# Two decoder layers on one core: part of layer 0's vector work moved to other engines, two key heads and two batches handled together

## The chip, the cores and the metric

The kernel runs on one core of a Trainium2 chip. The core has five engines with a queue each, worked off in order: TensorE (PE, with its weight loads PEld), VectorE (DVE), ScalarE (ACT), GpSimd (POOL) and SyncE (SP, which here only issues DMAs). The metric is the device time of one execution in microseconds (us); lower is better. Three runs of the kernel before gave 3500.85 us (median; 3487.28 to 3511.13).

## The reference, cut to what matters

The input is x, 16 batches of 256 tokens of width 256, in float32. Four blocks follow each other; each takes the layernorm of x and adds its result to x.

```python
x = x + attention0(layernorm(x))   # 32 query heads of 8 numbers, 8 key heads, rotary, causal softmax
x = x + experts(layernorm(x))      # a shared expert, and 8 others weighted by the two best logits
x = x + attention1(layernorm(x))   # gated delta rule, 16 heads of 128
x = x + ffn1(layernorm(x))         # gate, up and down weights are lut[index], a table of 16 values
```

For each token the experts give `shared(x) + sum over e of combine[e] * (silu(x @ Wg[e]) * (x @ Wu[e])) @ Wd[e]`, where `combine` is the softmax over the two best of 8 router logits and zero for the others. "Layer 0" below is the first two blocks, "layer 1" the third, "ffn" the last. The change is in layer 0 and in the layernorm helper, which the ffn uses too.

## The kernel before, in words

**Tiling.** x stays in SBUF as 32 tiles of 128 tokens; a batch is two tiles. Products that need more than one pass of 16 bits are made of pairs (a high part and the rest), three matmuls for each two halves of the rows (helper `three`, L114).

**Streams of layer 0.** Everything in layer 0 is written as generators that yield after each step. For each batch there are six: `prepare` (L402: layernorm, queries, keys, values), `greatest` (L461: the greatest score of each query), `attention` (L506), `ready` (L615: layernorm for the experts, then `route`, L564), `experts` (L622) and `to_gates` (L714: the next layer's layernorm and its decays and betas, `gates`, L293). Besides these run `lookups` (L189), which builds the ffn's weights with one-hot matmuls, and the loading of weights. `weave` (L54) issues their steps in the order of planned times in units of one batch: `STREAMS` at L723, with other times for the last two batches in `TAIL` (L725). A scheduler of the framework then places the instructions of each engine in its own order. That order is fixed when the program is built; an engine that waits holds up everything behind the waiting instruction.

**PSUM.** Layer 0 has 8 banks: 3 of role `s` (scores, routing), 3 of role `m` (projections, values, lookups, gates), 1 of role `e` (an expert's gate and up products, `pgu`) and 1 of role `y` (the experts' sum). So only one expert's `pgu` exists at a time, except for the last batch, whose `pgu` uses the three `s` banks.

**An expert** (`up`, L629; `down`, L649). TensorE makes `pgu` in 12 matmuls; ScalarE takes tanh of the gate half (L638); VectorE forms `(tanh + 1) * up` (L640) and times the gate (L641), which is the last to read `pgu`; GpSimd multiplies by the routing weight `cb`, which a DMA has spread over the partitions (L643; not for the shared expert); ScalarE rounds to float16 (L111) and VectorE takes the rest (L112), from SBUF; TensorE adds the two parts' products with the down weights into `ye` (L653). The next expert's `pgu` is issued before this expert's `ye`.

**Attention.** For each of 8 key heads, scores `t` are exponentiated twice by ScalarE (L519, L522), GpSimd subtracts (L523), and TensorE multiplies with the values into `po` (L533). VectorE then sums three parts (L536), inverts the sum of the weights (L539) and multiplies (L540), once for each key head.

**Layernorm helper** `normed` (L93): statistics on VectorE (L100 to L102), the power on GpSimd (L88), then one `tensor_scalar` of 256 elements for each tile on VectorE (L107), from SBUF to SBUF.

**Lookups** (L219 to L237). For each block of columns one matmul of 24 columns gives three parts of 8 results side by side (L234), and VectorE adds the three parts (L235).

**Routing and gates** are done for one batch at a time: 20 small VectorE instructions in `route`, most of 2 to 16 elements, 11 in `of` of `gates`.

Of the kernel before, what the change touches and what calls it, by code (L numbers as in the profile page):

```python
# [10 lines left out]
F32 = mybir.dt.float32  # L11
# [11 lines left out]
P = 128  # L23
B, S, D = 16, 256, 256          # batches, tokens of each, width
NT = B * S // P                 # 32 token tiles
NSB = NT // 4                   # 8 superblocks of 512 tokens
EPS = 1e-5
# layer 0 attention
H0, KV0, HD0 = 32, 8, 8
SC0 = HD0 ** -0.5  # L30
# layer 0 experts
NE, INTER0 = 8, 128
# layer 1 attention
# [3 lines left out]
XS = 2.0**12                    # scale of X and T of layer 1  # L37
WS, NS, OS, HS = 2.0**13, 2.0**10, 20.0, 0.5     # largest weight, and scales of the layernorms and of gated outputs, in pairs of float16
# [3 lines left out]
# layer 1 ffn  # L42
INTER1, NLUT = 688, 16
LOOKED_UP = (("gidx", INTER1, D), ("uidx", INTER1, D), ("didx", D, INTER1))      # rows and columns of the indices
# [9 lines left out]
def weave(*parts):  # L54
    """Issue some steps of each of several streams of work, each spread evenly over a part of the time."""
    turns = sorted((lo + (hi - lo) * (k + 0.5) / n, at, g) for at, (g, n, lo, hi) in enumerate((*x, 0, 1)[:4] if len(x) == 2 else x for x in parts) if g is not None for k in range(n))
    for _, _, g in turns:
        next(g, None)
# [3 lines left out]
def kernel(ctx: ExitStack, tc: tile.TileContext, a, out):  # L62
# [23 lines left out]
    def rsqrt_(t, n):  # L86
        """t [P, n] -> t ** -0.5, in place."""
        POOL.tensor_tensor(t, t, neghalf[:, :n], ALU.pow)  # L88
# [4 lines left out]
    def normed(pool, name, tiles, xn, scale):  # L93
        """xn = the layernorms of a few tiles, times scale."""
# [3 lines left out]
        rs = pool.tile([P, 4], F32, tag="ln_rs", name=f"rs_{name}", bufs=2)[:, :n]  # L98
# [5 lines left out]
        if scale != 1:  # L104
            DVE.tensor_scalar(rs, rs, scale, None, ALU.mult)
        for i, t in enumerate(tiles):
            DVE.tensor_scalar(xn[i], x[:, t, :], mv[:, i, 0:1], rs[:, i : i + 1], ALU.subtract, ALU.mult)  # L107

    def halve(pair, src):
        """pair = two of fewer bits that add up to src."""  # L110
# [3 lines left out]
    def three(ps, l, r):  # L114
        """ps = the products of the pairs l and r over both halves of their rows, less that of the low parts."""
# [4 lines left out]
    def normed_pair(pool, tiles, tag, bufs, bank, dt=F32R, scale=1):  # L120
        """Layernorms of two or four tiles, transposed, times scale, as a pair: [P, 2, 256 or 512]."""
# [17 lines left out]
    def greatest_of(p, bank, ts, name, sizes=()):  # L139
        """The greatest magnitude in each of a few lists of parts, whose rows have a size, on every partition: [P, n]."""  # L140
# [23 lines left out]
    def scales(p, most, name, bufs=2):  # L164
        """Of each weight, its scale, and the inverse of that and of the layernorms' scale."""
# [7 lines left out]
    def split(pair, t, scale):  # L173
        """pair = t times scale in two parts."""
# [3 lines left out]
    def now(g):  # L178
        """All of g at once; what it returns."""
# [6 lines left out]
    # ffn weights of layer 1, looked up on chip and kept in DRAM until they are used  # L186
    wl = {k: dram.tile([cols, rows], F32, tag=f"wl_{k}", name=f"wl_{k}") for k, rows, cols in LOOKED_UP}

    def lookups(pool, bank):  # L189
        """With a partition for each of 16 values and 8 parts of the rows, one or zero where a row's index is  # L190
        its value or not, times the value's entry in three parts: columns of the looked-up rows."""
# [9 lines left out]
        parts = small("parts", [R, 3], BF16)  # L201
        DVE.tensor_scalar(entry, entry, lut[:, 0:1], None, ALU.mult)
        DVE.tensor_copy(parts[:, :, 0], entry)
        DVE.tensor_tensor(rest, entry, parts[:, :, 0], ALU.subtract)
        DVE.tensor_copy(parts[:, :, 1], rest)
        DVE.tensor_tensor(parts[:, :, 2], rest, parts[:, :, 1], ALU.subtract)
# [12 lines left out]
        for name, rows, cols in LOOKED_UP:  # L219
            n = rows // R  # L220
            for c in range(0, cols, P):
# [4 lines left out]
                for k0 in range(0, n, step):  # L226
# [5 lines left out]
                    ps = bank(f"lk_{name}_{c}_{k0}")[:m, : ks * R * 3].rearrange("p (k r n) -> p r k n", k=ks, n=3)  # L232
                    for k in range(ks):
                        PE.matmul(ps[:, :, k, :], lhsT=hot[:, k * m : (k + 1) * m], rhs=parts, start=True, stop=True)  # L234
                    DVE.tensor_reduce(w[:, :, k0 : k0 + ks], ps, AX.X, ALU.add)  # L235
# [7 lines left out]
    # layernorms, transposed, in pairs; by head the decays of each position (zero for the first of a  # L243
    # chunk), and from the start of a chunk to each position
# [5 lines left out]
    def weights(j, p, one, stage):  # L250
        """Those of group j."""
# [15 lines left out]
        # of the values: no more than 1024 afterwards  # L267
# [20 lines left out]
        # scale of the gated outputs (no more than 2^16 then), and that of their products with the weights  # L288
# [4 lines left out]
    def gates(p, one):  # L293
        """What gives, for a batch, its part of beta, xd, al_d and dc_d."""
# [10 lines left out]

        def of(b):
            xT = normed_pair(p, range(2 * b, 2 * b + 2), "xT3", 1, one, F16, NS)
            for d, t in zip(xd[b // 2], xT):
                nc.sync.dma_start(out=d[:, :, b % 2 * S : b % 2 * S + S], in_=t)
            yield  # L310
            pz = one(f"gz_{b}")[:, : 4 * H1].rearrange("p (i n) -> p i n", i=2)
            for i in range(2):
                three(pz[:, i, :], [t[:, :, i * P : (i + 1) * P] for t in xT], bgk)
            parts = p.tile([P, 4, 2, 2 * H1], F32, tag="ga", name=f"ga_{b}", bufs=1)
# [934 lines left out]
```

## Time and profile before

| what | us |
|---|---|
| three runs, median (range) | 3500.85 (3487.28 to 3511.13) |
| profiled execution, its span from first to last instruction; no other time of it is given | 3504.0 |
| layer 0: until layer 1's first matmul | 1262 |
| last layer 0 attention output added to x (L560) | 1198.8 |
| last experts' output added to x (L664) | 1242.5 |
| layer 1: until the last output added to x (L1091) | 1262 to 3277 |
| ffn | 3278 to 3504 |
| VectorE busy, all | 2790.1 |
| TensorE busy, all | 2962.5 |
| ScalarE busy, all | 2107.7 |
| GpSimd busy, all | 1817.1 |

A group line of the profile reads: source line, engine, operation, tile written and tiles read, shapes, count; then busy time and mean ns of one instruction; then the idle time of that engine just before, and who ended it. A tile line gives shortest, median and longest duration in ns. A stage line (busy time of each engine in a stretch) gives the stretch, its length, then busy us and number of instructions of PE, PEld, DVE, ACT and POOL, then the granted TensorE clock as a share of full speed, the DMA engines' share and GB/s.

### The profile page before, as it was taken

What the parts mean: (1) busy time and instruction counts of PE and PEld (TensorE: products, weight loads), DVE (VectorE), ACT (ScalarE), POOL (GpSimd) and SP (SyncE); (2) the same over time, 40 slices, a digit from 0 to 9 for tenths busy, and PEclk for the clock granted to TensorE, in tenths of its full rate; (3) what the DMA queues carried; (4) which work ended last, traced back from release to release, by engine and by line L of the source; (5) the groups of instructions that cost most, each with busy time, mean ns of one, the idle gap of its engine ahead of it and who ended that gap; (6) DMA issues with size and microseconds to landing.
All of it is one profiled execution on the core that took longest, in us unless ns stands there. A gap on an engine that the chain in (4) does not pass through costs nothing.

```text
span 3504.0 us, 74239 instructions
## 1 busy us (share of the span) xinstructions
PE 2962.5 (85%) x28806; PEld 2346.1 (67%) x28806; DVE 2790.1 (80%) x5697; ACT 2107.7 (60%) x5131; POOL 1817.1 (52%) x1631
## 2 busy tenths in 40 slices
PE   3577877777778858989999899999989999999799
PEld 3356656556556636777777777777777777777688
DVE  4689988998889768888888888888888888887432
ACT  1455655555566536776776767676676676767332
POOL 2456555555556444555555555555555555554232
PEclk7789989999999968999999999999999999999899
DMA  6412222222232120111111111111111111110000
GB/s 178 134 58 69 76 74 76 82 68 81 73 81 53 34 69 16 55 52 47 34 40 39 57 48 36 40 32 52 42 51 40 32 40 35 37 35 13 25 25 25
DMA packets 175744, 188.60 MB, mean 54 GB/s; under 512 B 20734, under 2 KB 133214, under 8 KB 173662
## 3 DMA queue, kind: packets, MB, share of 16 engines
q1 hardware_dynamic: 166030, 167.07, 16.8%
q10 hardware_dynamic: 9360, 16.79, 1.6%
q8 instruction: 225, 3.69, 0.4%
q14 instruction: 129, 1.06, 0.1%
HBM read 150.14 MB, written 32.02 MB: 52 GB/s over the span
## 4 chain that ended last, share of the span: by engine, by line
PE 31%; DVE 19%; DMA 5%; ACT 4%; issue 2%; POOL 2%; SPq 0%; ACTq 0%; DVEq 0%; POOLq 0%
PE pr L850 5%; DMA Dm<-al_d 4%; DVE acc L865 3%; PE pq L899 3%; DVE Dm L932 3%; PE g L850 3%; DVE X L983 2%; PE Z L981 2%; DVE XT L961 2%; PE fg L118 2%; PE fu L118 2%; PE fy L777 2%; PE Y L975 2%; PE y L1089 2%; DVE XT L989 1%
## 5 line engine op out<-in xcount | busy, mean ns | idle before, releaser
L523 POOL TENSOR_TENSOR el<-e,eh 128x512 f16<-128x512 f32 x384 | 450.9, 1188 | 193.4 <-ACT eh L522 130.0
L865 DVE SCALAR_TENSOR_TENSOR acc<-pr,cv,acc 128x510 f32<-128x510 f32 (+2 forms) x384 | 281.2, 734 | 76.0 <-ACT acc L861 71.9
L519 ACT ACTIVATE e<-t 128x512 f32<-128x512 f32 x384 | 231.1, 603 | 139.5 <-PE t L517 70.4
L956 POOL TENSOR_TENSOR Tf<-Dm,kkm 128x512 f32<-128x512 f32 x128 | 161.7, 1282 | 246.7 <-DVE kkm L950 238.5
L983 DVE CAST_PREDICATED X<-masks,Z 128x512 f16<-128x512 uint8 x320 | 220.4, 689 | 67.3 <-PE Z L981 67.0
L522 ACT ACTIVATE eh<-t 128x512 f16<-128x512 f32 x384 | 229.0, 602 | 28.1 <-PE po L533 27.8
L1082 POOL TENSOR_TENSOR gl<-sg,gh 128x512 f16<-128x512 f32 x128 | 159.1, 1243 | 159.7 <-ACT gh L1081 156.3
L977 ACT ACTIVATE Y<-Y 128x512 f16<-128x512 f32 x320 | 191.1, 597 | 74.5 <-PE Y L975 73.4
L932 DVE TENSOR_TENSOR_SCAN Dm<-Dm,bI 128x512 f32<-128x512 f32 x128 | 184.2, 1440 | 56.9 <-DMA Dm<-al_d 53.0
L981 PE MATMUL Z<-Y,XT 128*128 128x64 f16 x2560 | 208.1, 249 | 24.5 <-ACT Y L977 20.6
L88 POOL TENSOR_TENSOR f<-f,neghalf 128x4 f32<-128x4 f32 x128 | 149.3, 1166 | 125.2 <-DVE f L1068 123.0
L981 PEld LDWEIGHTS <-XT 128*128 128x128 f16 x2560 | 176.1, 122 | 54.2 <-issue 31.8
L850 PE MATMUL pr<-xT,wqkv 128*128 128x512 f16 x768 | 208.2, 411 | 2.6 <-ACT v L907 2.6
L930 POOL TENSOR_TENSOR bI<-ident,beta 128x512 f32<-128x512 f32 x128 | 134.8, 1054 | 133.3 <-DVE Dm L932 100.4
L850 PEld LDWEIGHTS <-wqkv 128*128 128x128 f16 x1152 | 118.5, 111 | 119.7 <-issue 36.8
L850 PE MATMUL g<-xT,wga 128*128 128x256 f16 x1536 | 196.8, 279 | 1.9 <-DVE acc L865 0.8
L643 POOL TENSOR_TENSOR h<-h,cb 128x256 f32<-128x256 f32 x128 | 95.8, 749 | 192.9 <-DVE h L641 77.7
L515 PE MATMUL t<-Qt,Kt 128*128 128x512 bf16 x384 | 150.8, 402 | 51.9 <-DVE nm L486 31.3
L1089 PE MATMUL y<-woa,gh 128*128 128x256 f16 x1024 | 183.0, 275 | 8.0 <-ACT gh L1081 5.7
L975 PE MATMUL Y<-X,Th 128*128 128x64 f16 x2560 | 145.6, 202 | 44.2 <-DVE X L983 33.9
L486 DVE TENSOR_REDUCE nm<-s 128x2 f32<-128x512 f32 x256 | 171.7, 677 | 13.7 <-PE s L485 13.2
L989 DVE STREAM_TRANSPOSE XT<-X 128x512 f32<-128x512 f32 x256 | 179.6, 702 | 1.9
(362 smaller groups left out, 9930.9 us busy)
## 6 DMA issues: line engine op xcount, KB each, us to landing
Dm<-al_d SPq DMA_DIRECT2D x128, 256.0 KB
cb<-cd SPq DMA_DIRECT2D x128, 128.0 KB
dB<-dc_d ACTq DMA_DIRECT2D x64, 256.0 KB
xT<-xd SPq DMA_DIRECT2D x64, 256.0 KB
Qt<-qd SPq DMA_DIRECT2D x32, 408.0 KB
qd<-both SPq DMA_DIRECT2D x32, 192.0 KB
xr_gidx<-ix_gidx SPq DMA_DIRECT2D x34, 160.0 KB
xr_uidx<-ix_uidx SPq DMA_DIRECT2D x34, 160.0 KB
```

The costliest lines, as they stand in the source:

```text
L519: ACT.activation(e32, ps, AF.Exp, scale=SC0)
L522: ACT.activation(eh[n], ps, AF.Exp, scale=SC0)
L523: POOL.tensor_tensor(el[n], e32, eh[n], ALU.subtract)
L850: PE.matmul(ps, lhsT=r if flip else l, rhs=l if flip else r, start=k == 0, stop=k == len(todo) - 1)
L865: DVE.scalar_tensor_tensor(to[:, :, d:], frm[:, :, : S - d], w["cv"][:, ct, 3 - d : 4 - d], to[:, :, d:], ALU.mult, ALU.add)
L932: DVE.tensor_tensor_scan(flat(Dm[c]), flat(Dm[c]), flat(bI), 0.0, ALU.mult, ALU.add)
L975: PE.matmul(py[:, c, h, :], lhsT=Th[c][:, h, :], rhs=even(X)[:, h, :, :, c], start=True, stop=True)
L977: ACT.activation(Y, py, AF.Copy, scale=XS**-2)
L981: PE.matmul(pz[:, h, :, c], lhsT=XT[:, h, :, c], rhs=Y[:, c, h, :], start=True, stop=True)
L983: DVE.copy_predicated(even(X).rearrange("p h n e c -> p h n (e c)"), bcast(odd[s_].rearrange("p (n e) c -> p n (e c)", e=s_), 1, G), split ...
L989: DVE.transpose(words(XT), words(X))
L1089: PE.matmul(py, lhsT=pair[m][:, h, :], rhs=w["wo"][n][:, h, :], start=k == 0, stop=k == len(todo) - 1)
```

## The change

Line numbers of the new version are about 5 to 30 higher. It does the following:

1. `normed`: VectorE makes `shift = -mean * rs` in one small instruction for each call, and ScalarE makes `x * rs + shift` for each tile (activation Identity with a bias and a scale taken from SBUF); the VectorE instruction L107 is gone, here and in the ffn.
2. `lookups`: the three parts are added by TensorE, three matmuls of 8 columns in place of one of 24; ScalarE copies the sum out of PSUM in place of VectorE's sum.
3. `values` of the attention: two key heads share one PSUM bank; one sum, one inverse (written back into PSUM) and one product for both.
4. `ready`, `route` and `gates` take one batch, (0), then six pairs (1,2) to (11,12), then 13, 14 and 15 each alone.
5. `experts`: GpSimd's product with `cb` comes before VectorE's second product, whose result is written into the up half of `pgu` in PSUM; ScalarE and VectorE make the two float16 parts from there. So `pgu` is in use until L112 is done, not until L641.
6. The planned times of `ready`, `experts`, `gates` and of the last four batches change.

```diff
-        rs = pool.tile([P, 4], F32, tag="ln_rs", name=f"rs_{name}", bufs=2)[:, :n]
+        rs, shift = (pool.tile([P, 4], F32, tag=f"ln_{k}", name=f"{k}_{name}", bufs=2)[:, :n] for k in ("rs", "shift"))
...
+        DVE.scalar_tensor_tensor(shift, mv[:, :n, 0], -1.0, rs, ALU.mult, ALU.mult)
         for i, t in enumerate(tiles):
-            DVE.tensor_scalar(xn[i], x[:, t, :], mv[:, i, 0:1], rs[:, i : i + 1], ALU.subtract, ALU.mult)
+            ACT.activation(xn[i], x[:, t, :], AF.Identity, bias=shift[:, i : i + 1], scale=rs[:, i : i + 1])
...
                     for k in range(ks):
-                        PE.matmul(ps[:, :, k, :], lhsT=hot[:, k * m : (k + 1) * m], rhs=parts, start=True, stop=True)
-                    DVE.tensor_reduce(w[:, :, k0 : k0 + ks], ps, AX.X, ALU.add)
+                        for h in range(3):
+                            PE.matmul(ps[:, k], lhsT=hot[:, k * m : (k + 1) * m], rhs=parts[:, h], start=h == 0, stop=h == 2)
+                    ACT.copy(w[:, :, k0 : k0 + ks], ps.rearrange("p k r -> p r k"))
...
-            def values(g, eh, el):
-                po = bank(f"po_{b}_{g}", "v")[:, :200].rearrange("p (i h n) -> p i h n", i=2, h=4)
+            def values(g, eh, el, po):
+                g2 = g % 2
...
+                if g2 == 0:
+                    return
...
-                DVE.reciprocal(rinv, po[:, :, :, 0])
+                DVE.reciprocal(po[:, :, :, 0], po[:, :, :, 0])
+                at = 32 * (g - 1)
                 DVE.tensor_tensor(
-                    on[:, :, 32 * g : 32 * g + 32].rearrange("p i (h d) -> p i h d", d=8), sums, bcast(rinv, 3, 8), ALU.mult)
+                    on[:, :, at : at + 64].rearrange("p i (h d) -> p i h d", d=8), sums, bcast(po[:, :, :, 0], 3, 8), ALU.mult)
...
-        def route(b, xT):
+        def route(bs, xT):
...
                 DVE.scalar_tensor_tensor(h, h, 1.0, pgu[:, 1], ALU.add, ALU.mult)
-                DVE.scalar_tensor_tensor(h, pgu[:, 0], 0.5 * HS / (WS * NS) ** 2, h, ALU.mult, ALU.mult)
                 if e < NE:
                     POOL.tensor_tensor(h, h, cb, ALU.mult)
+                DVE.scalar_tensor_tensor(pgu[:, 1], pgu[:, 0], 0.5 * HS / (WS * NS) ** 2, h, ALU.mult, ALU.mult)
                 pair = [p.tile([P, S], F16, tag=f"h{m}", name=f"h{m}_{b}_{e}") for m in range(2)]
-                halve(pair, h)
+                halve(pair, pgu[:, 1])
...
-        STREAMS = ((prepare, 7, -3.4, -2.4), (greatest, 26, -1.7, -0.55), (attention, 34, 0, 0.9), (ready, 5, 1.3, 1.75), (experts, 28, 1.75, 2.65), (to_gates, 3, 2.65, 3.15))
+        STREAMS = ((prepare, 7, -3.4, -2.4), (greatest, 26, -1.7, -0.55), (attention, 34, 0, 0.9))
+        TOGETHER = [(0,)] + [(b, b + 1) for b in range(1, B - 3, 2)] + [(b,) for b in range(B - 3, B)]
+        READY, EXPERTS, GATES = (5, 1.15, 1.5), (28, 1.5, 2.4), (3, 3.3, 3.8)
+        TAIL = {
+            B - 4: ((1.15, 1.5), (1.5, 2.35), (3.2, 3.6)), B - 3: ((1.3, 1.6), (2.2, 2.95), (2.95, 3.2)),
+            B - 2: ((1.25, 1.5), (1.95, 2.6), (2.6, 2.8)), B - 1: ((0.97, 1.15), (1.6, 2.2), (2.2, 2.4))}
         LOOK, LOAD, EXW, GTW = (120, 1, 16), (26, 5, 16), (31, -2.4, 1), (3, 1, 1.2)
-        TAIL = {B - 2: ((1.2, 1.5), (1.5, 2.3), (2.3, 2.6)), B - 1: ((0.95, 1.1), (1.1, 1.9), (1.9, 2.2))}
...
+        for bs in TOGETHER:
+            b, n = bs[-1], len(bs)
+            (r0, r1), (e0, e1), (g0, g1) = TAIL[b] if b in TAIL else (READY[1:], EXPERTS[1:], GATES[1:])
+            todo.append((ready(bs), READY[0], b + r0, b + r1))
+            for k in range(n):
+                at = b + e0 + k * (e1 - e0)
+                todo.append((experts(bs[k]), EXPERTS[0], at, at + e1 - e0))
+            todo.append((to_gates(bs), GATES[0], b + g0, b + g1))
```

## The prediction

> **What bounds the kernel now.** I read the stage table first, since the change only touches layer 0 and the layernorms of the ffn. Columns: stretch, length, then busy us of PE, PEld, DVE, ACT, POOL.
>
> ```profile
> 0.00:263.00 263.00, 147.99 (x1261) 106.94 (x1262) 172.75 (x406) 97.14 (x185) 112.55 (x113) 0.79 0.44 123
> 263.00:1139.00 876.00, 696.61 (x7438) 524.64 (x7437) 780.67 (x2077) 503.93 (x1024) 507.69 (x481) 0.93 0.27 73
> 1139.00:1262.00 123.00, 85.99 (x829) 64.26 (x827) 79.92 (x249) 57.66 (x122) 50.12 (x56) 0.85 0.16 43
> 1262.00:3278.00 2016.00, 1820.71 (x18066) 1465.76 (x18066) 1670.47 (x2779) 1378.68 (x3685) 1075.04 (x925) 0.96 0.13 40
> 3278.00:3504.00 226.00, 211.15 (x1216) 184.52 (x1216) 86.32 (x189) 70.25 (x117) 71.66 (x59) 0.95 0.09 29
> ```
>
> In the main stretch of layer 0, 263 to 1139, VectorE is busy 781 of 876 us (89%), TensorE 80%, ScalarE and GpSimd 58%. In the ffn TensorE is busy 93% and VectorE 38%: what VectorE saves there (32 instructions L107) buys nothing. Layer 1 is not touched. So the question is what layer 0's 1262 us become.
>
> Second, the groups of instructions inside layer 0.
>
> ```profile
> L523 POOL TENSOR_TENSOR el<-e,eh 128x512 f16<-128x512 f32 x384 | 450.9, 1188 | 193.4 <-ACT eh L522 130.0
> ...
> L112 DVE TENSOR_TENSOR h<-h,h 128x256 f16<-128x256 f32 x144 | 87.1, 605 | 22.7 <-ACT h L111 22.3
> ...
> L540 DVE TENSOR_TENSOR on<-sums,rinv 128x64 f32<-128x64 f32 x128 | 71.0, 555 | 0.3
> L107 DVE TENSOR_SCALAR xn_xT<-x,mv_xT,rs_xT 128x256 f32<-128x256 f32 x96 | 63.6, 701 | 3.6 <-POOL el L523 1.3 <-PE xnp_xT L131 1.1 <-POOL rs_xT L88 0.8
> ...
> L536 DVE TENSOR_REDUCE sums<-po 128x64 f32<-128x192 f32 x128 | 44.0, 344 | 1.5 <-PE po L533 1.3
> ```
>
> Third, the expert's own tile (shortest/median/longest ns), because the change lengthens the use of the only `pgu` bank.
>
> ```profile
> L638 ACT ACTIVATE h<-pgu,half_down x144: 448/473/624, 225.6 to 1235.8; 128x256 f32<-128x256 f32 x144
> L640 DVE SCALAR_TENSOR_TENSOR h<-h,pgu x144: 356/408/423, 227.1 to 1236.5; 128x256 f32<-128x256 f32 x144
> L641 DVE SCALAR_TENSOR_TENSOR h<-pgu,h x144: 361/412/425, 227.6 to 1238.1; 128x256 f32<-128x256 f32 x144
> L111 ACT CAST h<-h x144: 387/406/550, 228.4 to 1239.6; 128x256 f16<-128x256 f32 x144
> L112 DVE TENSOR_TENSOR h<-h,h x144: 351/416/1856, 229.0 to 1240.9; 128x256 f16<-128x256 f32 x144
> L643 POOL TENSOR_TENSOR h<-h,cb x128: 717/727/922, 233.3 to 1238.6; 128x256 f32<-128x256 f32 x128
> ...
>   POOL h L643: 75.2, 39
> ...
>   PE pgu L118: 23.2, 21
> ```
>
> Two things are seen. L112 and L640 have the same 256 elements; L640 and L641, with an operand in PSUM, never take over 425 ns, L112, all in SBUF, takes up to 1856, a mean of 605. The surplus is about the 1188 ns of one GpSimd instruction L523: VectorE instructions of this kind stand still while GpSimd works. L540 (203/496/1667) and L107 (352/414/1810) show the same. And the first `pgu` product of the next expert starts in the middle case 0.33 us after L641 ends (start times of the trace): the one bank is reused at once.
>
> **The change part by part, VectorE in layer 0** (busy 172.75 + 780.67 + 79.92 = 1033 us).
> - L107 goes: −63.6. `shift` for 36 calls (16 `prepare`, 10 `ready`, 10 `gates`, where 48 calls were): nearest row L318, a small product of two SBUF tiles, 436 ns: +16. Twelve calls fewer also save L102 and L105 (256 and 469 ns): −9.
> - L235 goes: 9.8 + 8.9 + 8.8 = −27.5.
> - Two key heads at once: L536, L539 and L540 cost 44.0 + 24.6 + 71.0 = 139.6. After: 64 times (sum: L235 shows 120 elements in 260 ns against 192 in 344, so 1.2 ns an element, 344 + 230 = 574; inverse 200; product 203 + 67 = 270, free of the standing still because one operand is in PSUM) = 67. −72. If the product still stands still: 64 x (555 + 67) = 40 instead of 17, so −49 at least.
> - Routing: the 20 instructions of one batch sum to 6.4 us, gates' 11 to 3.4 us; six calls fewer of each, less the longer rows (0.5 and 0.4 each): −35 and −18.
> - L112 reads PSUM: 144 x (605 − 412) = −28. [...]
>
> Sum: −63.6 + 16 − 9 − 27.5 − 72 − 35 − 18 − 28 = −237 us, bounds −200 and −250: VectorE falls to about 796.
>
> **What the others get.** ScalarE: 96 scalings; tanh with one scale from SBUF takes 475 for 256 elements, and L861 (scale from SBUF, 512 elements) takes 84 more than L519 (none), so a second operand makes 560: +54. 110 copies like L319 (258) : +28. Table loads fall from 34 to 22 in the program, 12 x 1.283 = −15; fewer gates −8. Sum +59 on 659. That is 61% of the time forecast below, so it is hidden, except in the layernorm's own chain (560 for 414 ns). TensorE: 536 matmuls become 1608; five of them took 0.28 us in the timeline, the first 0.175, so 26 ns each: 1072 x 0.026 = +28 (each alone: 175 ns, +188; they follow each other, so 28). GpSimd: 12 powers fewer, −9. SP's queue: 18 DMAs fewer; `cd` goes out once for two batches. Its loads of `cb` wait there for GpSimd's product to free the buffer (188.5 us, 65 times, in the waits of SP), and others stand behind them; that product comes earlier in an expert now, so this wait doesn't grow by the change alone.
>
> **What is lengthened.** (a) `pgu` stays in use through GpSimd's product, L641, L111 and L112. In the undisturbed expert at 1202.1 the next `pgu` came 3.04 us after this one, with L112 ending 1.62 us after that. So the least cycle is 3.04 + 1.62 and a wake of 0.05 = 4.7 us. (b) VectorE now waits for GpSimd in the middle of an expert; today that wait (75.2 us, 39 times) is ScalarE's. Behind it on VectorE stand the `nm` sums that free the score banks, and TensorE waits for those. (c) A pair is routed only when its second batch has its attention, so experts come later: in TensorE's order 20 experts stand behind the last attention output instead of 13.
>
> **Sum, by the expert's cycle.** Experts follow each other without gap because of the one bank, so they are the clock of layer 0. Before: 225.6 to 1199 for 131 experts, 7.43 us each; the unhindered cycle is 3.0, so 4.4 us of it is queueing at four hand-overs. After: the order of each engine in the built programs shows four experts in every pair of batches (18) with nothing else on TensorE between them; those take 4.9. For the other 14: between L640 and L641 two VectorE instructions stand in both programs (median), between L641 and L112 seven before and two after, 0.38 us each on average (780.67/2077). Part of that runs beside GpSimd's and ScalarE's own shares of the chain, so I take 0.4 us of queueing at each of seven hand-overs: 4.7 + 2.7 = 7.4. At the pair's end gates wait for the experts, about 3 us. So (14 x 7.4 + 4 x 4.9 + 3)/18 = 7.0 us. Attention ends at 225 + 124 x 7.0 = 1093 instead of 1199. Behind it: 11 experts on the one bank x 4.9 = 54, six more of the last batch on three banks x 2.3 (today's nine take 21.8) = 14, a rest of 2: 70 us where 1199 to 1243 were 44. Then 19 us to layer 1, as before. Layer 0 ends at 1182 instead of 1262: −80.
>
> Can TensorE follow? Of its 697 us in the main stretch, 7 experts (15 us) move behind the attention and 28 come: 710 us, in 876 − 106 = 770 us: 92%, where layer 1 reaches 90%. At 90% the stretch takes 789, attention ends at 1112, layer 0 at 1201: −61. [...] Weight loads are 525 + 28 − 9 = 544 us, 71% of 770, where layer 1 shows 73%: at 73% the stretch could go down to 745, layer 0 to 1157: −105. Busy time says that −80 is a little too much, weight loads that it is not. I take the middle of −80 and −61: the profiled execution at 3504 − 71 = 3433; it lies 3 us above the median of the runs, so 3430.
>
> **The rivals.**
> 1. *The bank eats the gain.* The change then does what it says to VectorE, and it buys nothing. With 0.5 us at each of the seven hand-overs instead of 0.4 the 14 take 8.2, the mean is 4.9 x 4/18 + 8.2 x 14/18 + 0.2 = 7.6: 225 + 124 x 7.6 + 89 = 1256, −6: 3495. One tenth of a us for each hand-over is the whole gain. For it: the 0.33 us after which the bank is reused today. Against: the tighter order, and a VectorE at 68%.
> 2. *Slower.* VectorE waits for GpSimd (b), whose product may stand behind L523 (1188 ns) or a late `cb` (22.8 us in all today), and the `nm` sums wait with it, then TensorE's scores. It decides at 124 x c + 314 = 1262, c = 7.65; 0.6 us a hand-over makes 8.9 and c = 8.2: 225 + 1017 + 89 = 1331, +69: 3570. For it: seven hand-overs for four, and today each costs 1.1. Against: VectorE has 237 us to spare, and the wait is 75 today.
> 3. *More.* At 0.25 us a hand-over the 14 take 6.45, the mean 6.3: 225 + 781 + 89 = 1095; weight loads allow 1157 or, at TensorE's ffn share of 82% (184.52/226), 663 for the stretch. Between 1110 and 1150: about 3375. [...] Against: 80% busy today.
>
> **Numbers.** Forecast 0.48, rival 1 0.25, rival 2 0.17, rival 3 0.10. About 1% (35 us) is what a measurement of this kernel can tell from no change. The forecast (c from 6.75 to 7.35, so 3390 to 3464) and rival 3 are faster: 0.58; rival 1 is the same: 0.25; rival 2 slower: 0.17. The range of 8 in 10 goes from 3375 (half of rival 3 lies below) to 3540 (most of rival 2 lies above); the forecast's own is 3390 to 3464.
>
> **What would show it.** Right: VectorE near 795 busy in layer 0; L112 of the experts near 0.41 without long ones; the mean from tanh to tanh near 7.0 until the last attention output, which lands near 1093 to 1112; 70 us behind it. Wrong: VectorE idle before the second gate product, with GpSimd named, over 75 us; TensorE idle before `pgu`, with L112 named, over 100 us; or a layer 1 or ffn that moves by over 10 us.

## The result, and the profile after

The changed kernel took 3654.4 us (median of four runs, 3651.0 to 3658.2), the kernel before 3500.5 us beside it: ratio 1.044, 95% interval 1.0414 to 1.0466. It is 4.4% slower. The forecast was 3430, the range ended at 3540. The profiled execution has a span of 3649.2 us; it is 145 us longer than that of before. The stage table shows where (columns as in the prediction):

```profile
0.00:263.00 263.00, 152.28 (x1406) 108.79 (x1407) 162.40 (x380) 111.04 (x218) 118.70 (x118) 0.81 0.45 126
263.00:1295.00 1032.00, 798.35 (x8721) 591.72 (x8721) 655.80 (x1626) 549.72 (x1206) 517.50 (x491) 0.86 0.23 63
1295.00:1385.00 90.00, 61.33 (x413) 42.84 (x410) 39.76 (x130) 27.97 (x61) 15.12 (x21) 0.83 0.12 31
1404.00:3419.00 2015.00, 1814.05 (x18066) 1462.54 (x18066) 1667.55 (x2782) 1379.98 (x3685) 1073.89 (x925) 0.96 0.14 40
3419.00:3649.00 230.00, 213.73 (x1216) 185.59 (x1216) 76.16 (x165) 85.86 (x149) 70.52 (x59) 0.95 0.09 28
```

Layer 1 took 2015 us (2016 before), the ffn 230 (226). All of the loss is in layer 0: the last attention output lands at 1294.6 instead of 1198.8 (+96), and from there to the last experts' output it takes 90 instead of 44 us (+46). In the main stretch (263 to 1295) no engine is busy for most of the time any more: VectorE 656 of 1032 us (64%; it was 89%), TensorE 77%, ScalarE and GpSimd 53 and 50%. So the added time is waiting, and the question is for what.

The expert's own instructions are as short as foretold. Shortest, median and longest ns, by the tile `h`:

```profile
L653 ACT ACTIVATE h<-pgu,half_down x144: 449/474/609, 216.8 to 1380.5; 128x256 f32<-128x256 f32 x144
L655 DVE SCALAR_TENSOR_TENSOR h<-h,pgu x144: 359/421/423, 217.3 to 1381.5; 128x256 f32<-128x256 f32 x144
L658 DVE SCALAR_TENSOR_TENSOR pgu<-pgu,h x144: 360/426/433, 218.4 to 1382.8; 128x256 f32<-128x256 f32 x144
L112 ACT CAST h<-pgu x144: 350/373/442, 219.2 to 1383.3; 128x256 f16<-128x256 f32 x144
L113 DVE TENSOR_TENSOR h<-pgu,h x144: 386/416/426, 220.0 to 1383.7; 128x256 f16<-128x256 f32 x144
L657 POOL TENSOR_TENSOR h<-h,cb x128: 718/726/939, 223.1 to 1382.0; 128x256 f32<-128x256 f32 x128
```

L113 (L112 before) has no long ones left: 426 at most, where it had 1856. But look at the waits of layer 0 in the kernel after (who waited, for whom; us in total, times, longest):

```profile
POOL h L657 <- DVE h L655: 197.4, 63, 8.6
ACT h L653 <- PE pgu L119: 171.8, 102, 5.3
DVE h L655 <- ACT h L653: 156.2, 88, 5.3
...
ACT h L112 <- DVE pgu L658: 93.3, 57, 3.6
...
PE ye L668 <- ACT h L112: 72.8, 43, 2.6
...
DVE pgu L658 <- POOL h L657: 43.5, 45, 3.8
```

Each step of the expert is named as what the next engine sat idle for. In the kernel before the same view has only these of the expert among its first eight rows:

```profile
POOL h L643 <- DVE h L641: 77.7, 34, 11.2
ACT h L111 <- POOL h L643: 75.2, 39, 5.8
ACT h L638 <- PE pgu L118: 70.9, 62, 3.7
```

An engine that sits idle for one step of the expert has that step next in its fixed order, and what stands behind it waits too: in the 63 waits before L657 GpSimd ran nothing for 197.4 us. From the start times of the trace: from one expert's tanh to the next it took 8.7 us on average until the attention ended (216.8 to 1294.6 for 124 experts), where before had 7.43.

### The profile page after: what moved, and what is told of

Read it like the earlier page. It is cut to its first block, busy times and chain, and to the rows that moved or that the text cites. A ratio compares the mean times of both kernels' runs of the same rounds, so it can differ in the third digit from the quotient of the medians.

```text
span 3649.2 us, 75907 instructions
## 1 busy us (share of the span) xinstructions
PE 3042.2 (83%) x29836; PEld 2392.7 (66%) x29836; DVE 2607.0 (71%) x5101; ACT 2159.5 (59%) x5327; POOL 1800.7 (49%) x1619
## 4 chain that ended last, share of the span: by engine, by line
PE 30%; DVE 19%; DMA 5%; ACT 5%; issue 2%; POOL 2%; SPq 0%; ACTq 0%; DVEq 0%; POOLq 0%
DMA Dm<-al_d 5%; PE pr L878 4%; DVE acc L893 3%; PE pq L927 3%; DVE Dm L960 3%; PE g L878 3%; DVE X L1011 2%; DVE XT L989 2%; PE Z L1009 2%; PE fy L805 2%; PE fg L119 2%; PE fu L119 2%; PE Y L1003 2%; PE y L1117 2%; DVE XT L1017 1%
## 5 line engine op out<-in xcount | busy, mean ns | idle before, releaser
L528 POOL TENSOR_TENSOR el<-e,eh 128x512 f16<-128x512 f32 x384 | 442.2, 1168 | 230.4 <-ACT eh L527 136.4
L657 POOL TENSOR_TENSOR h<-h,cb 128x256 f32<-128x256 f32 x128 | 94.1, 735 | 315.9 <-DVE h L655 197.4
L1110 POOL TENSOR_TENSOR gl<-sg,gh 128x512 f16<-128x512 f32 x128 | 158.7, 1240 | 155.7 <-ACT gh L1109 155.3
L668 PE MATMUL ye<-w_wd,h 128*128 128x256 f16 x864 | 159.3, 301 | 76.9 <-ACT h L112 72.8
```

The costliest lines, as they stand in the source:

```text
L528: POOL.tensor_tensor(el[n], e32, eh[n], ALU.subtract)
```

## The experiments

All kernels ran beside the kernel before. "Attention ends" and "layer 0" are the starts of the VectorE instructions that add the last attention output and the last experts' output to x, in the profiled execution; "behind" is the rest of its span. Numbers 1 to 5 are the parts of the change as listed above; change 6, the planned times, goes with 4. These three columns come from one execution of each kernel. It lies 13 to 19 us below the median in swap, no4no5 and no5_no3, and 8 and 11 us above it in two_banks and two_no5_no1, so differences of less than about 20 us in them (an estimate from these) are to be read with the medians beside them.

| run | contains | median us | ratio (95% interval) | attention ends | layer 0 | behind |
|---|---|---|---|---|---|---|
| before | - | 3500.5 | | 1198.8 | 1242.5 | 2261.5 |
| after | 1 2 3 4 5 | 3654.4 | 1.044 (1.0414 to 1.0466) | 1294.6 | 1384.9 | 2264.3 |
| no5 | 1 2 3 4 | 3404.2 | 0.9747 (0.9711 to 0.9784) | 1138.2 | 1191.1 | 2207.5 |
| no4 | 1 2 3 5 | 3660.6 | 1.0463 (1.0444 to 1.0483) | 1389.8 | 1442.1 | 2218.9 |
| no4no5 | 1 2 3 | 3519.0 | 1.0049 (1.0026 to 1.0071) | 1203.1 | 1241.6 | 2261.8 |
| only5 | 5 | 3620.0 | 1.0346 (1.0321 to 1.0371) | 1299.5 | 1354.7 | 2263.9 |
| swap | 1 2 3 4, order of 5 | 3501.7 | 0.9998 (0.9977 to 1.002) | 1165.0 | 1227.0 | 2260.1 |
| two_banks | after, two banks | 3500.2 | 1.0007 (0.9983 to 1.0032) | 1182.5 | 1230.0 | 2276.4 |
| no4_cb8 | no4, 8 `cb` | 3714.4 | 1.0647 (1.0584 to 1.0711) | 1391.5 | 1437.4 | 2272.8 |
| no4_nmT | no4, `nmT` in `m` | 3533.3 | 1.0092 (1.0073 to 1.0111) | 1271.3 | 1320.4 | 2207.5 |
| after_nmT | after, `nmT` in `m` | 3562.2 | 1.017 (1.0117 to 1.0222) | 1255.5 | 1344.8 | 2213.5 |
| only2 | 2 | 3450.3 | 0.9865 (0.9831 to 0.9899) | 1209.9 | 1250.4 | 2198.6 |
| twice_on | before, L540 twice | 3531.6 | 1.0089 (1.0062 to 1.0115) | 1232.6 | 1274.7 | 2261.6 |
| no5_no1 | 2 3 4 | 3403.1 | 0.9717 (0.9703 to 0.9732) | 1139.9 | 1191.1 | 2206.1 |
| no5_no3 | 1 2 4 | 3437.1 | 0.9805 (0.9775 to 0.9834) | 1156.1 | 1207.3 | 2208.8 |
| two_no5 | no5, two banks | 3407.2 | 0.9728 (0.9688 to 0.9769) | 1160.2 | 1204.1 | 2199.1 |
| two_no5_no1 | 2 3 4, two banks | 3407.6 | 0.9733 (0.9689 to 0.9777) | 1177.1 | 1219.5 | 2197.5 |

The last column falls into two groups, 2197 to 2219 and 2260 to 2276, in a layer 1 that no run touches. The section on it is below; until then read the column "layer 0".

### Which part of the change costs the time

Theory A was change 5 (the chain through the one `pgu` bank), theory B change 4 (pairs and their planned times), theory C one of changes 1 to 3. Four runs undo 4 and 5 in all combinations.

no5 puts the old order back (no4 sets `TOGETHER` to single batches and the planned times of before; no4no5 does both; only5 is the kernel before with the reverse of this diff):

```diff
                 DVE.scalar_tensor_tensor(h, h, 1.0, pgu[:, 1], ALU.add, ALU.mult)
+                DVE.scalar_tensor_tensor(h, pgu[:, 0], 0.5 * HS / (WS * NS) ** 2, h, ALU.mult, ALU.mult)
                 if e < NE:
                     POOL.tensor_tensor(h, h, cb, ALU.mult)
-                DVE.scalar_tensor_tensor(pgu[:, 1], pgu[:, 0], 0.5 * HS / (WS * NS) ** 2, h, ALU.mult, ALU.mult)
...
-                halve(pair, pgu[:, 1])
+                halve(pair, h)
```

> After with change 5 undone: VectorE makes both products from PSUM, then GpSimd, then the two parts from SBUF, so pgu is free at the second product. Theory A (the serial chain of seven hand-overs through the one pgu bank made after slow): the cycle from tanh to tanh falls from 8.4 to 8.7 us to under 7.4; attention ends before 1198.8 us and the time is below the kernel before, 3400 to 3480. Theory B (pairs and their plan, change 4): the attention still ends near 1290 and the time stays at 3600 to 3650. Theory C (one of changes 1 to 3): also 3600 to 3650.

> After with change 4 undone: ready, route and gates for each batch alone, planned times of before. Changes 1, 2, 3 and 5 stay. Theory A: the chain is still there, the cycle stays above 8 us, 3580 to 3680. Theory B: 3400 to 3500, the tail back from 90 to 44 us and the attention end under 1200. If the two share the loss, the 46 us of the tail go and the 96 us of the attention stay: 3600.

> Only changes 1, 2 and 3. Theories A and B alike: VectorE has some 160 us less to do and nothing is lengthened but ScalarE's scaling of the layernorm: 3400 to 3480. Theory C: slower than before by 50 us or more, 3550 to 3650.

> The kernel before with change 5 alone. Theory A: the chain meets a VectorE that is busier than in after, so the hand-overs cost more than there: 3620 to 3720, the cycle 8.5 to 9.3 us. Theory B or C: within 1 % of before, 3470 to 3530.

Theory A holds, B and C fall. Layer 0 with changes 1 to 3: 1241.6; with 4 added 1191.1 (−51); with 5 added 1442.1 (+200); with both 1384.9 (+143). Change 5 costs 112 us in the kernel before, 200 beside changes 1 to 3, 194 beside 1 to 4. Change 4, suspected, gains. And changes 1 to 3 together, which relieve VectorE, gain 0.9 us of layer 0 in the profiled execution, and by the medians the kernel is 18 us slower than before: theories A and B alike had expected 3400 to 3480 there, and it took 3519. So the relief of VectorE, on which the prediction counted, bought nothing there. Theory A missed once, too: it expected change 5 to cost more beside the busier VectorE of only5, with a cycle of 8.5 to 9.3 us; it costs least there, and the cycle until the attention ends is 8.3.

### Which half of change 5

swap keeps the new order but puts the product into SBUF, so the bank is free at VectorE's second product. two_banks keeps all of after and gives `pgu` a second bank at the cost of one of role `m`.

```diff
-                DVE.scalar_tensor_tensor(pgu[:, 1], pgu[:, 0], 0.5 * HS / (WS * NS) ** 2, h, ALU.mult, ALU.mult)
+                DVE.scalar_tensor_tensor(h, pgu[:, 0], 0.5 * HS / (WS * NS) ** 2, h, ALU.mult, ALU.mult)
...
-PS0_BUFS = {"s": 3, "m": 3, "e": 1, "y": 1}
+PS0_BUFS = {"s": 3, "m": 2, "e": 2, "y": 1}
```

> After, but the second gate product goes into the SBUF tile h instead of the up half of pgu; GpSimd's product stays between VectorE's two. So pgu is free at the second product, after five hand-overs in place of seven. If the number of hand-overs that hold the bank sets the loss (layer 0 ends at 1192 without change 5 and at 1386 with it), one more than without should cost about a third: layer 0 ends at 1230 to 1300, the time is 3490 to 3570. If VectorE standing behind GpSimd in the middle of an expert is the loss, nearly all of it stays: layer 0 ends above 1350, 3610 or more.

> After with two banks for pgu instead of one, and two for role m (projections, values, lookups, gates) instead of three. If the one bank is the bound, an expert can start while the one before is still in its chain: layer 0 ends below 1250 instead of at 1386, time 3460 to 3520. If the engines' order or the planned times are the bound, it still ends above 1330, 3590 or more. A bank less for role m may cost some of it.

In swap layer 0 ends at 1227.0: the order alone, GpSimd between VectorE's two products, costs 36 us of the 194 (1227.0 − 1191.1; the profiled execution of swap lies 13 us below its median, and the medians less "behind" give 45), less than the third that was expected. The hold of the bank from the second product to L113, with all that hangs on it, costs the rest, some 150 to 158. With two banks layer 0 ends at 1230.0: 155 of the 194 come back. The waits of layer 0 (until 1240) in swap and in two_banks:

```profile
ACT h L653 <- PE pgu L119: 91.7, 79, 3.6
...
DVE h L655 <- ACT h L653: 55.2, 54, 3.4
PE pgu L119 <- DVE h L658: 39.0, 27, 3.1
DVE h L658 <- POOL h L657: 35.5, 40, 3.9
```

```profile
ACT h L112 <- DVE pgu L658: 102.0, 65, 10.8
ACT h L653 <- PE pgu L119: 95.3, 69, 7.2
...
DVE h L655 <- ACT h L653: 44.3, 38, 4.0
```

VectorE's wait for the tanh, 156.2 in after, is 55.2 and 44.3; ScalarE's wait for `pgu`, 171.8, is 91.7 and 95.3. In two_banks ScalarE still waits 102 us for the second product (93 in after) and yet layer 0 is 155 us shorter: another expert's `pgu` can be made meanwhile.

### What else lives in that bank

Why does change 5 cost 88 us more in no4 than alone? The waits of no4 show one that only5 does not have (its window is 250 to 1300 us):

```profile
PEld L520 <- DMA Qt<-nd: 117.0, 13, 15.0
PE t L520 <- DMA Qt<-nd: 112.9, 13, 14.7
```

The first theory was SP's queue: loads of `cb` wait there for GpSimd's product to free one of two buffers (188.5 us before, 362.9 in after, 88 times), and Qt's load stands behind them. no4_cb8 gives `cb` eight buffers.

> The run without change 4 (changes 1, 2, 3 and 5) with eight buffers instead of two for cb, so that SP's loads of cb need not wait for GpSimd and nothing stands behind them. There Qt's load was waited for 113 us by TensorE, 13 times; the kernel before with change 5 alone has no such wait and ends layer 0 some 88 us earlier. If SP's queue is the cause of these 88 us, the wait goes below 20 us and layer 0 ends at 1340 to 1380 instead of at 1443. If it is not, layer 0 ends above 1420. Layer 1's instructions stand in the order of the kernel before here, not in that of the run without change 4, so the time is the end of layer 0 plus 2261: 3600 to 3640, or 3680 and more.

That theory falls. In no4_cb8 the wait is still there, and layer 0 ends at 1437.4:

```profile
PE t L520 <- DMA Qt<-nd: 133.8, 12, 14.7
```

The second theory comes from the order of the instructions. `nmT`, the transposed negated maxima of the scores, goes by two DMAs (`nd`, then `Qt`) into the operand of the scores `t` of its batch. And `nmT` uses the bank of the experts: PS0_ROLE gives its tag "n" the role `e`, which the description ahead of the prediction left out. Counted in the traces, so many TensorE instructions stand between `nmT` and the first `t` of its batch: from the second batch on 106 to 274 in the kernel before, 90 to 222 in only5, but 17 to 23 in no4 from the fifth batch on, and in after 43, 59, 52, 63, 45, 21 and 17 in every second one. With so little between them, TensorE waits until the two DMAs have landed: in eight of these twelve batches of no4 13 to 18 us pass from `nmT` to `t`. Why the scheduler places `nmT` so late was not shown: only5 holds the bank as long, and its `nmT` is not late.

no4_nmT and after_nmT change one letter:

```diff
-PS0_ROLE = {"s": "s", "t": "s", "p": "m", "n": "e", ...
+PS0_ROLE = {"s": "s", "t": "s", "p": "m", "n": "m", ...
```

> The run without change 4 (changes 1, 2, 3 and 5), with nmT, the transposed negated maxima that Qt's load waits for, in a bank of role m instead of the one bank e that the experts use. In the run without change 4 only 17 TensorE instructions stand between nmT and the first scores t of the same batch in 12 of 16 batches (about 200 in the kernel before), so the way of nmT through two DMAs lies open, 13 waits, 113 us. Here 200 to 248 stand between. If that is what made it slower than change 5 alone: no wait for Qt, layer 0 ends at 1330 to 1365 instead of at 1442, and with layer 1 in the same order as there (2219 us behind it) 3550 to 3585. If not: above 1420, 3640 and more.

> After with nmT in a bank of role m instead of the experts' bank e; 173 to 321 TensorE instructions stand between nmT and the first scores of its batch from the third batch on, where in after every second batch has 17 to 63. If the late nmT is most of change 5's cost in pairs (194 us of layer 0), layer 0 ends at 1230 to 1270. If the experts' chain through the bank is most of it, only the 42 us of waits for Qt and a little more go: layer 0 ends at 1320 to 1350. The cost of change 5 alone in the kernel before, where nmT is not late, was 112 us, which speaks for the second.

no4_nmT ends layer 0 at 1320.4 instead of 1442.1 (−122, no wait for Qt left among its waits), 10 us more than expected; after_nmT, as expected, at 1344.8 instead of 1384.9 (−40). In swap and in two_banks, too, `nmT` is not late (113 to 412 and 153 to 330 places ahead of its `t`, from the second batch on), so what they give back contains its cost. Of after's loss by change 5 (194 us) 40 are then the late `nmT` and 36 the order of the products; the rest, 118 by subtraction, is the experts' chain that holds the bank. The three were not measured in one kernel, and their sum need not be exact.

### Layer 1 that nobody touched

no5 gains 105 us in the profiled execution, 51 in layer 0 and 54 behind it. In the traces the order of TensorE's 18,048 instructions in layer 1 differs from that of before in 11,953 places in no5, no4, no4_nmT, no5_no1, no5_no3, two_no5 and two_no5_no1, in 11,915 in only2, and in 0 to 41 in only5, no4no5, after, swap, two_banks, no4_cb8 and twice_on (after_nmT has a third order, 11,490). It is the same program text; where layer 0 changes, the framework's scheduler can place layer 1 in another order. only2 is the test: change 2 alone, with 27 us less for VectorE and 28 more for TensorE.

> The kernel before with change 2 alone (the lookups' three parts added by TensorE, copied by ScalarE). VectorE has 27 us less, TensorE 28 more: layer 0 ends at 1225 to 1250 (1242.5 before). The built program has layer 1 in the same order of instructions as the run without change 5, which took 2206 us from the last experts' output to the end where before takes 2261. If that order is what is worth 54 us, this run shows it too: 3430 to 3455. If the gain there came from something in layer 0 (clock, heat, transfers), this run stays at 3480 to 3505.

It takes 3450.3, −50, while its layer 0 is 8 us later than before. Layer 1 and the ffn in only2:

```profile
1270.00:3222.00 1952.00, 1780.73 (x18066) 1448.41 (x18066) 1653.43 (x2777) 1382.86 (x3685) 1067.22 (x922) 0.98 0.14 41
3222.00:3449.00 227.00, 211.30 (x1217) 184.56 (x1216) 87.93 (x190) 70.23 (x117) 72.15 (x61) 0.95 0.08 29
```

Before: 2016 us, 1820.71 busy on TensorE at a granted clock of 0.96. With the other order the same 18,066 matmuls are busy 1780.73 at 0.98, and TensorE is idle 171 instead of 195 us (1952 − 1781, 2016 − 1821). Whether fewer gaps make the higher clock, or the reverse, no run here shows. All nine kernels with the second or third order have 2197 to 2219 us behind layer 0, all eight with the first, before and after among them, 2260 to 2276. after_nmT agrees: against after, one letter for layer 0 changes the order of layer 1, and "behind" falls from 2264 to 2214. An engineer who sees only2's 50 us as the gain of change 2 would be wrong.

### What VectorE's time is worth

The prediction took the relief of VectorE as what makes each hand-over cheaper. Three runs ask what VectorE's time is worth in itself.

```diff
                 DVE.tensor_tensor(
                     on[:, :, 32 * g : 32 * g + 32].rearrange("p i (h d) -> p i h d", d=8), sums, bcast(rinv, 3, 8), ALU.mult)
+                DVE.tensor_tensor(
+                    on[:, :, 32 * g : 32 * g + 32].rearrange("p i (h d) -> p i h d", d=8), sums, bcast(rinv, 3, 8), ALU.mult)
```

> The kernel before with VectorE's product on<-sums,rinv (L540, 128 times, mean 555 ns) made twice in a row: 71 us more work for VectorE and nothing else; the result is the same. If VectorE's busy time is what layer 0 waits for, as the prediction has it, layer 0 ends 60 to 71 us later, at 1300 to 1315, and the time is 3560 to 3575. If VectorE's busy time has slack and the chains between the engines set the pace, it ends less than 25 us later: 3500 to 3525.

no5_no1 puts L107's `tensor_scalar` back in place of `shift` and the ScalarE activation; no5_no3 puts the old `values` back.

> Changes 2, 3 and 4: the run without change 5 with the layernorm's scaling back on VectorE. Layer 1 stands in the same order as in the run without change 5 (layer 0 1191, time 3404). If taking 64 us from VectorE helps there, this is later by 20 to 60 us: layer 0 1210 to 1250, 3425 to 3465. If the longer way of the layernorm through ScalarE (590 for 414 ns, and ScalarE's queue) costs as much as it gives: 1170 to 1200, 3385 to 3415.

> Changes 1, 2 and 4: the run without change 5 with one sum, one inverse and one product for each key head again, which is 72 us more for VectorE by the prediction's working. Layer 1 stands in the same order as in the run without change 5. If VectorE's time counts: layer 0 1220 to 1260, 3435 to 3475. If holding a bank of role m over two heads costs what the fewer instructions give: 1180 to 1205, 3395 to 3420.

twice_on lies between its two cases: VectorE's busy time in layer 0 grows by 53 us (1033.5 to 1086.3) and layer 0 ends 32 us later. no5_no1 ends layer 0 at 1191.1, where no5 does, and its median is the same (3403.1 against 3404.2): change 1 buys nothing, although it takes 25 us of busy time from VectorE in layer 0 (901.8 without it, 877.1 with it, until layer 1's first matmul). no5_no3 is 16 us later in layer 0 of the profiled execution, which lies 19 us below its median, and 33 us later by the median, for 39 us of busy time there (916.2 against 877.1): its two expectations were not told apart by that. So a us of VectorE was worth about 0.6 us in the kernel before (32 of 53), and in no5 nothing (change 1) or 0.4 to 0.8 (change 3). Change 3 also changes how long a bank of role `m` is held, so its gain need not be VectorE's time alone.

Was the one bank what hid the rest? two_no5 is no5 with two banks for `pgu`, two of role `m`, and `nmT` in role `y`; two_no5_no1 the same without change 1.

> Changes 1 to 4 (the run without change 5), with two banks for pgu, two of role m instead of three, and nmT in the bank of role y. Layer 1 stands in the same order as in the run without change 5. If the one bank sets the pace of layer 0 even without change 5, layer 0 ends at 1120 to 1170 instead of at 1191, and the time is 3330 to 3380. If other chains do, or the missing bank of role m costs as much: 1185 to 1215, 3395 to 3425.

> The same with the layernorm's scaling on VectorE (changes 2, 3 and 4). If the one bank hid what change 1 takes from VectorE, this is later than the run with two banks and change 1 by 20 us or more. If VectorE's busy time has slack in any case, the two are within 10 us in layer 0.

No: layer 0 of two_no5 ends at 1204.1, 13 later than no5. Without change 5 the single bank is not the bound, or the bank taken from role `m`, or `nmT` in role `y`, costs as much; these runs do not tell that. two_no5_no1 is 15 us later in layer 0 of the profiled execution, but its median is the same (3407.6 against 3407.2): unclear.

no5 and no5_no1, at 3404 and 3403 us, are the fastest versions found, 2.5 to 2.8% under the kernel before; about half of that is layer 1's order.

## Why the prediction was wrong

**The step that failed** is "I take 0.4 us of queueing at each of seven hand-overs: 4.7 + 2.7 = 7.4" (seven times 0.4 is 2.8, a slip of 0.1), with the four quiet experts of 4.9 that made it c = 7.0. Measured over experts 9 to 120, from the end of one step to the start of the next: 0.29 us before the tanh, 0.42 before L655, 0.38 before GpSimd, 0.51 before L658, 0.77 before the cast, 0.60 before L113, 0.88 until the next `pgu`: 3.85, or 0.55 each. A few long waits make these means; the medians are 0.03 to 0.58. The steps take 1.83 for `pgu` and 0.474 + 0.421 + 0.726 + 0.426 + 0.373 + 0.416 = 2.84: 4.67, the 4.7 of the prediction. Together 8.5, and 8.4 as measured, since the shared experts pass no GpSimd.

**The relief hardly reached the hand-overs of the long chain.** The prediction let the queueing fall from 1.1 to 0.4 us a hand-over because VectorE has less to do. The same measurement in four kernels (us per expert, means of experts 9 to 120, from the start of one `pgu` to that of the next):

| kernel | VectorE relieved | hand-overs | steps | queueing | cycle |
|---|---|---|---|---|---|
| before | no | 4 | 3.1 | 4.6 | 7.7 |
| no5 | yes | 4 | 3.0 | 3.9 | 6.9 |
| only5 | no | 7 | 4.6 | 3.9 | 8.5 |
| after | yes | 7 | 4.6 | 3.8 | 8.4 |

With the long chain the queueing is nearly the same with the relief (3.8 in after, 3.6 in after_nmT, where no late `nmT` adds to it) and without it (3.9 in only5), and for one hand-over it is about half of what it is in the short chain. So in these kernels it did not grow with the number of hand-overs, and the relief took at most 0.3 us of it in the long chain; what sets it stays open. What the change added in full are the steps that now lie inside the hold of the bank: GpSimd's product, the cast and L113, 1.5 us for an expert. From no5 to after the cycle grows by 1.5 us, which for the 135 experts on the one bank makes some 200 us (an estimate from these means), the size of change 5's 194.

**The quiet experts hardly existed.** The middle cycle of after is 7.4 us, nine in ten take over 5.5, and 3 of 123 take 5.0 or less, where four in eighteen were to take 4.9. Behind the attention, too, the expert's cycle was 5.6 (seven cycles, 1316.9 to 1356.3) where 4.9 was assumed, and 90 us passed where 70 were foretold. With 8.4 instead of 7.4 for the other fourteen the sum would have given 7.8; without quiet experts it gives 8.4. One gap makes it the 8.7 of the result: after the first batch's nine experts the first pair waits for the attention of its second batch, and for 48 us no `pgu` is made. The prediction had the late experts of a pair, under (c), but not this gap.

**The single bank had a second user.** The prediction named the bank, but only with `pgu` in it. The late `nmT` costs 40 us in after and 122 in no4. It could have been read from the order of the built program: the count of instructions between `nmT` and `t`.

**VectorE falls to 796: wrong, and its value too.** The sum of the removed durations was right: the durations of VectorE's instructions in layer 0 fall from 1215.7 to 977.9, −237.8 for −237. But busy time falls from 1033.5 to 863.3, −170. In the trace a VectorE instruction's record begins about 78 ns before the end of the one ahead when they follow each other (the middle case of before's layer 0; 81 in after); 182 us of before's durations overlap so, 115 of after's. The prediction subtracted durations from a busy time, which counts the overlap once. For a small instruction such as L102 of before (256 ns), 78 ns are about a third of its duration, and they are no gain. And busy time taken away did not turn into time one for one, as twice_on and no5_no1 show: 89% busy in the main stretch was no proof that VectorE bounds it.

**What was right.** The parts of VectorE, in the kernel after:

```profile
L544 DVE TENSOR_REDUCE sums<-po 128x128 f32<-128x384 f32 x64 | 35.0, 547 | 2.0 <-PE po L539 2.0
L549 DVE TENSOR_TENSOR on<-sums,po 128x128 f32<-128x128 f32 x64 | 17.7, 277 | 0.7
L106 DVE SCALAR_TENSOR_TENSOR shift_xT<-mv_xT,rs_xT 128x2 f32<-128x2 f32 (+1 forms) x36 | 16.8, 465 | 2.4 <-POOL rs_xT L88 1.9
L547 DVE RECIPROCAL po<-po 128x16 f32<-128x16 f32 x64 | 16.4, 256 | 0.6
```

Sum, inverse and product of two heads: 35.0 + 17.7 + 16.4 = 69, 67 foretold; `shift` 16.8, 16 foretold. The product has lost its long waits (277 ns a mean), as an operand in PSUM let expect. L113 from PSUM takes 416 in the middle case and 426 at most, and L112 took 416 in the middle case from SBUF: the row was right; 27 us went, 28 foretold. The bound of −200 leaves room for an L112 that is slower from PSUM, which no run shows. The scaling on ScalarE takes 597, 560 foretold; ScalarE in all has 35 us more in layer 0 (693.7 against 658.7), not the 59 of the sum. TensorE in layer 0: 1014 for 931 us, of which 28 were foretold for the matmuls; the no5 run, with the same matmuls at a clock of 0.89 instead of 0.84, has 944, +13. That TensorE can reach layer 1's shares in layer 0 (90% busy, 73% of the time in weight loads), on which the −61 and the −105 rest, was the author's estimate, and no run shows it: in no5, whose main stretch is the shortest (263 to 1138), they are 85% and 65% (747.16 and 570.56 of 875 us). Layer 1 and the ffn moved by 3 us together (2264.3 against 2261.5). None of the prediction's signs of being wrong came up: VectorE's wait for GpSimd in mid-expert is 43.5 us (75 was the sign), TensorE's wait for L113 before `pgu` 6.2 (100), and layer 1 and the ffn moved by less than 10. The loss lay in the sum of many short waits, which no one of these signs looked at.

**The rivals.** Rival 2 had the direction, the point from which it decides (c = 7.65) and nearly the cycle (8.2 for 8.7), with a chance of 0.17. Its mechanism was only in part the right one: the wait for GpSimd is worth 36 us (swap), while the hold of the bank through the cast and L113, which the prediction listed under (a) as 4.7 us instead of 3.04, was the large piece. The sentence that SP's wait for `cb` would not grow was wrong, 188.5 became 362.9, but in no4 that wait cost nothing (no4_cb8).

## What to carry to other kernels

Where a single buffer is handed through a chain of engines, add up the steps between its first write and its last read: what was moved into that hold was paid in full here (1.5 us for an expert), and queueing should not be counted down for a relief elsewhere that no run has shown (3.8 us here with it, 3.9 without). Then ask who else uses the buffer, and how far in each engine's order its product stands from its use (17 to 23 instructions in no4, and the late `nmT` cost 122 us). Don't subtract durations from busy time (here 237.8 us of durations were 170 of busy time), and don't take a high busy share for a bound: add a known amount of work to the engine and see what comes out (in twice_on 53 us more of VectorE's busy time made layer 0 32 us longer). Compare stages, not totals: a change can reorder a stage it does not touch, and here that was worth 54 us, about what change 4 gains.

## What the hardware showed that was not expected

**VectorE instructions that stand still beside GpSimd.** The prediction inferred this from L112's long ones, whose surplus is up to 1440 ns (1856 − 416) and not only the 1188 of one L523. The trace of before shows it instruction by instruction: of L112's 144 executions, 65 met no GpSimd instruction (under 20 ns in common with one), and none of these took over 426 ns; the 79 that did took 767 on average. Of L540's 128, 32 met none and took 226 at most; the other 96 took 670. The 144 of L641, with an operand in PSUM, took 425 at most, though 70 met GpSimd.

The loss also moves on when its victims are removed. L540 doubled should add 71 us (128 × 555 ns). In layer 0 of twice_on, and then of the kernel before:

```profile
L112 DVE TENSOR_TENSOR h<-h,h 128x256 f16<-128x256 f32 x144 | 82.0, 570 | 20.1 <-ACT h L111 19.8
L542 DVE TENSOR_TENSOR on<-sums,rinv 128x64 f32<-128x64 f32 x128 | 68.1, 532 | 0.7
L540 DVE TENSOR_TENSOR on<-sums,rinv 128x64 f32<-128x64 f32 x128 | 67.1, 524 | 0.4
```

```profile
L112 DVE TENSOR_TENSOR h<-h,h 128x256 f16<-128x256 f32 x144 | 87.1, 605 | 22.7 <-ACT h L111 22.3
L540 DVE TENSOR_TENSOR on<-sums,rinv 128x64 f32<-128x64 f32 x128 | 71.0, 555 | 0.3
```

Both copies have a mean far above their median of 225 ns, and L112 is a little shorter. In no5, where L107 and most of L540's long ones are gone, the same instruction L113 from SBUF got longer instead, 721 ns for 605:

```profile
L113 DVE TENSOR_TENSOR h<-h,h 128x256 f16<-128x256 f32 x144 | 103.7, 721 | 54.6 <-ACT h L112 54.5
```

So 17 us of what was taken away came back at the next instruction with all operands in SBUF. The long durations belong to the meeting with GpSimd more than to the instruction that shows them.

**The granted clock in layer 0.** Until layer 1's first matmul, in before, no5, two_banks and after (stage lines as above; the clock is the third number from the end):

```profile
0.00:1262.00 1262.00, 930.59 (x9524) 695.83 (x9524) 1033.34 (x2731) 658.73 (x1329) 670.35 (x648) 0.89 0.30 81
0.00:1208.00 1208.00, 943.61 (x10554) 712.08 (x10554) 880.06 (x2156) 693.42 (x1493) 662.17 (x633) 0.89 0.31 84
0.00:1247.00 1247.00, 961.84 (x10554) 726.63 (x10554) 866.03 (x2156) 692.58 (x1493) 652.29 (x633) 0.87 0.29 81
0.00:1404.00 1404.00, 1014.41 (x10554) 744.60 (x10554) 863.29 (x2156) 693.69 (x1493) 656.27 (x636) 0.84 0.26 72
```

The same matmuls of layer 0 are busy 944 us in no5 and 1014 in after, at a lower clock. In the main stretch the clock is 0.93 in before and no5, 0.86 in after and no4, and 0.89 in only5. It is lowest where the waits are longest, but their share does not set it alone: in two_banks TensorE is busier than in before (77% of layer 0 against 74%), and its clock is lower. What lowers the clock, and how much of the 194 us it makes, no run here separates.
